# Identity products in TensorE's waits, the next norm inside the output part, and the last 64 rows by rows: a four-layer f32 attention kernel

## The chip, the cores and the metric

One core of a Trainium2 chip. The metric is the device time of the kernel in microseconds (us); all data are f32. Before the change the median of three runs is 2748.88 us (2748.11 to 2750.48).

The engines are called as the profile calls them: PE (TensorE, the matrix products; PEld is its weight load), DVE (VectorE), ACT (ScalarE), POOL (GpSimd), and SP, which in this kernel issues the DMAs in one queue. [...] A product of f32 operands is two matrix instructions (two passes) in the profile.

## The reference

Four layers work one after the other on `x` (8, 100, 512); each also reads the context `ctx` (8, 361, 512).

```python
x = gqa(x, ctx, mask)         # L0: 32 heads over 8 key heads, residual, layer norm
x = time_mix(x, ctx[:, ...])  # L1: norm, shift, five gated mixes, a scan over the 100 rows
                              #     (32 heads of 16x16 states), norm per head, residual;
                              #     then ln2, shift, and x + sigmoid(xr @ Wr) * (relu(xk @ Wk)**2 @ Wv)
x = x + alpha * attend(x, ctx, w_q, w_k, w_v, w_o)       # L2: one head of 512
for i in (1, 2):                                         # L3: two cross-attentions
    h  = layer_norm(x, ln_i)
    q  = h @ wq + bq                                     # 16 heads of 128
    k  = concat(ctx @ wk + bk, bias_k)                   # 361 + 1 keys
    v  = concat(ctx @ wv + bv, bias_v)
    w  = softmax(q k^T / sqrt(128))
    x  = x + (w v) @ wo + bo
x = x + gelu(layer_norm(x) @ w_fc1 + b_fc1) @ w_fc2 + b_fc2   # 512 -> 2048 -> 512
```

## The kernel before, in words

The first layer fills 0 to about 300 us of the profiled span, the second and third layer (interleaved, in units of two batches) 300 to 830, the last layer's cross-attentions 830 to 2570, its MLP the rest.

*Second and third layer.* PE's order is written by hand: generators (`prescan`, `mixing`, `after` and others) yield pieces, and an order of pieces is laid out so that one unit's products stand in another's waits. The rest of the engines are ordered by the tile scheduler from program order and readiness. `normed` (line 553) normalizes rows and turns them by products with the identity into a bank `pn`; `through` (line 598) takes a 512x512 weight through a bank `pp`; `prescan` takes the mix through `w1` into a bank `pt` (line 617). The scan is on DVE (`st<-wd,a`, 1.83 us each) and POOL.

*Last layer.* Four steps, (layer 1, 2) x (half 0, 1), a half being four batches, 400 columns. All engines are ordered by the scheduler. Each step has these parts:

- `project_queries` (L1160): for pairs of heads, `seven_products` (L1120, a two-by-two block product with seven instead of eight products, whose operands' sums are made beforehand on POOL and DVE and whose results are combined on DVE) gives `pq`, then q, and `through_keys` multiplies q by the head's key weight, so that `qz` holds 512 values for each of 16 heads x 100 rows = 1600 rows of a batch. The sums of the input `hT`, called `hs`, are four additions on DVE at its head (L1172 to 1175). While pair h is projected, pair h-2 goes through the keys (`some_keys`); in the first pair there is nothing for that place.
- `attend` per batch (L1212): 12 tiles of 128 rows in pairs, and 64 rows left. For a pair of tiles, `pair_of_scores` (L1272) makes sums `ss` on POOL (`sums`, L1237) and seven products with the context, then softmax on DVE and ACT, transposes, and `block_with_context` (L1289) multiplies by the context with seven products. The parts of the latter wait in a list (`waiting`) and are put between the scores' products (`meanwhile`). The last 64 rows of two batches share one softmax; `with_context` (L1247) multiplies each batch's 64 columns by the context with four column parts, three key blocks each, two to a bank `pz`, and evicts them to `qz` (L1342 to 1350).
- the next half's `normalize` (L1473): `take_rows` loads its four row blocks `xin`, statistics and normalization on DVE, transposes on PE (`pt<-ident,xhat`, line 128), ACT writes `hT`.
- `project_outputs` (L1390): first `take_rows` loads the rows to which the result is added. For pairs of heads, `pa` by the value weight, `u` (the value bias and the bias key's weight, loaded from `pd`) added on DVE into `aT`, POOL makes `sums` of `aT` and the output weights, and the pair before goes through the seven output products `po`, added on DVE to seven accumulators `acc` and `more` (L1425). After the last pair, the accumulators are added up (L1427), turned on PE (`pt<-ident,more`, line 1466), added to the rows on DVE (L1467), and stored by SP (`put_rows`).

PSUM banks and SBUF tiles rotate by tag; `l3_ctx` and `l3_out` are pools on the same side of SBUF, opened one after the other.

## Time and profile before

| what | value |
|---|---|
| median of the runs | 2748.88 us |
| the profiled execution's own time | 2747.97 us |
| its span, first to last instruction | 2745.9 us |
| mean granted clock of PE | 0.983 |
| PE busy | 2621.6 us, 95% |
| DVE busy | 1605.1 us, 58% |
| POOL busy | 1042.8 us, 38% |
| ACT busy | 935.8 us, 34% |

The busy shares are of the span. The row of clocks gives the TensorE clock granted in tenths of full speed, in 40 slices of 68.6 us. The waits of an engine are listed as `engine line waited for: us in total, times, longest us`. In a timeline, each line is start, duration, engine, line, operation, and in brackets the idle time before it with the instruction that ended it. A line of a table of stretches gives the stretch, its length, then busy time and count of PE, PEld, DVE, ACT and POOL, the mean granted clock, the DMA share and GB/s.

### The profile page before, as it was taken

The numbers are of one execution on the slowest core, as the hardware profiler recorded it, in microseconds if no ns is written. First come the engines' busy times: TensorE is split into PE (matmuls) and PEld (weight loads), VectorE is DVE, ScalarE is ACT, GpSimd is POOL, SyncE is SP. The second block draws the span as 40 slices with busy tenths as digits, with TensorE's granted clock in tenths as the row PEclk, the third lists the DMA queues.
The fourth block names the chain that finished last, engine by engine and source line by source line (L and its number), as shares of the span: only waits on it lengthen the run. The fifth ranks groups of instructions, "written<-read, shape, count | busy, mean of one in ns | idle before, by whom it ended". The sixth has DMA issues, their size and how long they took to land.

```text
span 2745.9 us, 40332 instructions
## 1 busy us (share of the span) xinstructions
PE 2621.6 (95%) x14356; PEld 2093.8 (76%) x14356; DVE 1605.1 (58%) x3995; ACT 935.8 (34%) x2143; POOL 1042.8 (38%) x1362
## 2 busy tenths in 40 slices
PE   8999888888989999999999999999999999999999
PEld 5666466666666888877788877789887788886688
DVE  4788366877524656546556546555554655654743
ACT  5777334543321333310233330243331143331121
POOL 2000144532204445355345446344546334535212
PEclk9999889999999999999999999999999999999999
DMA  7432333354205100045200035400015510005400
GB/s 228 119 102 74 121 110 123 94 151 121 81 26 154 51 23 23 7 130 161 78 23 23 1 91 149 127 19 23 12 38 147 148 43 23 23 7 162 155 13 13
DMA packets 149682, 220.63 MB, mean 80 GB/s; under 512 B 45302, under 2 KB 78646, under 8 KB 149226
## 3 DMA queue, kind: packets, MB, share of 16 engines
q1 hardware_dynamic: 149482, 218.05, 27.5%
q8 instruction: 114, 1.87, 0.3%
q14 instruction: 86, 0.70, 0.1%
HBM read 207.48 MB, written 10.53 MB: 79 GB/s over the span
## 4 chain that ended last, share of the span: by engine, by line
PE 67%; POOL 4%; DVE 3%; DMA 2%; issue 1%; ACT 1%; SPq 0%; DVEq 0%; POOLq 0%; ACTq 0%
PE pz L97 18%; PE sl L97 9%; PE pk L1168 6%; PE su L97 5%; PE pq L97 5%; PE po L1416 5%; PE pa L97 5%; PE pp L97 3%; PE pu L97 3%; PE pt L1336 2%; PE pl L97 2%; DMA xin<-xd 1%; PE sc L1377 1%; PE sc L97 1%; POOL ss L1241 1%
## 5 line engine op out<-in xcount | busy, mean ns | idle before, releaser
L97 PE MATMUL pz<-at,cr 121*128 121x256 f32 (+1 forms) x960 | 255.3, 378 | 0.0
L751 POOL TENSOR_TENSOR st<-st,r 128x800 f32<-128x800 f32 x64 | 111.8, 1748 | 233.5 <-DVE st L745 195.3
L1311 DVE TENSOR_TENSOR qz<-pz,qz 128x512 f32<-128x512 f32 x192 | 131.9, 687 | 113.7 <-PE pz L97 105.8
L97 PEld LDWEIGHTS pz<-at,cr 121*128 121x128 f32 (+1 forms) x960 | 177.5, 189 | 21.0
L1168 PE MATMUL pk<-q,wb 128*128 128x400 f32 x512 | 189.9, 501 | 3.1 <-issue 3.1
L97 PE MATMUL pa<-qz,wa 128*128 128x400 f32 x512 | 178.2, 499 | 0.1
L97 PE MATMUL sl<-ts,ss 128*128 128x181 f32 x768 | 156.5, 325 | 3.7 <-POOL ts L1233 0.2
L97 PE MATMUL pz<-at,cs 121*128 121x256 f32 (+1 forms) x576 | 149.7, 380 | 0.0
L1241 POOL TENSOR_TENSOR ss<-qz 128x256 f32<-128x256 f32 x96 | 69.8, 727 | 207.1 <-PE su L97 118.4
L97 PEld LDWEIGHTS pa<-qz,wa 128*128 128x128 f32 x512 | 96.2, 190 | 64.9 <-DVE aT L1454 0.9
L1091 ACT COPY qz<-pk 128x400 f32<-128x400 f32 x128 | 63.0, 492 | 236.0 <-PE pk L1168 236.0
L1339 ACT COPY at<-pt 121x384 f32<-121x384 f32 x192 | 84.2, 480 | 159.2 <-PE pt L1336 94.1
L1358 ACT ACTIVATE pr<-su,nm 128x362 f32<-128x362 f32 x96 | 54.1, 564 | 239.4 <-DVE nm L1354 239.3
L97 PEld LDWEIGHTS sl<-ts,ss 128*128 128x128 f32 x768 | 118.2, 190 | 21.3 <-issue 7.1
L1168 PEld LDWEIGHTS pk<-q,wb 128*128 128x128 f32 x512 | 93.6, 190 | 50.5 <-ACT qz L1091 3.7
L350 PEld LDWEIGHTS pt<-ident,pr 115*121 115x121 f32 (+1 forms) x672 | 83.2, 185 | 56.5 <-ACT at L230 29.2
L745 DVE TENSOR_TENSOR_SCAN st<-wd,a 128x808 f32<-128x808 f32 x64 | 117.0, 1828 | 14.7 <-PE py L756 12.9
L1361 ACT ACTIVATE pr<-pr,ss 128x362 f32<-128x362 f32 x200 | 113.5, 595 | 31.7 <-DVE ss L1359 31.6
L342 ACT ACTIVATE pr<-pr,nm 115x361 f32<-115x361 f32 (+1 forms) x224 | 115.2, 592 | 10.4 <-DVE nm L338 10.4
L97 PEld LDWEIGHTS pz<-at,cs 121*128 121x128 f32 (+1 forms) x576 | 104.4, 189 | 13.7 <-issue 1.8
L338 DVE CUSTOM_DVE_ANT_0 pr<-sc,mask 115x361 f32<-115x361 f32 (+1 forms) x224 | 106.0, 530 | 11.0 <-PE sc L326 10.8
L350 PE MATMUL pt<-ident,pr 115*121 115x115 f32 (+1 forms) x672 | 99.9, 280 | 11.0 <-ACT at L230 5.4
(383 smaller groups left out, 6241.1 us busy)
## 6 DMA issues: line engine op xcount, KB each, us to landing
va<-vd SPq DMA_DIRECT2D x64, 404.0 KB
wa<-in_L_xattn_wq SPq DMA_DIRECT2D x64, 256.0 KB
wb<-in_L_xattn_wk SPq DMA_DIRECT2D x64, 256.0 KB
wa<-in_L_xattn_wv SPq DMA_DIRECT2D x64, 256.0 KB
wb<-in_L_xattn_wo SPq DMA_DIRECT2D x64, 256.0 KB
u<-pd SPq DMA_DIRECT2D x64, 200.0 KB
cr<-in_ctxR SPq DMA_DIRECT2D x16, 726.0 KB
cx<-in_ctxT SPq DMA_DIRECT2D x16, 722.0 KB
```

The costliest lines, as they stand in the source:

```text
L97: nc.tensor.matmul(dst, lhsT=lt, rhs=r, start=(i == 0), stop=(i == len(pairs) - 1))
L338: nc.vector.tensor_tensor_reduce(out=pr[:n], in0=sc[:n, :S], in1=mk[t][:n], scale=-1.0, scalar=FLT_MAX, op0=ALU.add, op1=ALU.min, accum_ou ...
L342: nc.scalar.activation(pr[:n], pr[:n], AF.Exp, bias=nm[:n], scale=-1.0)
L350: nc.tensor.transpose(pt[:KB, k * n : (k + 1) * n], pr[:n, lo : lo + KB], ident[:n, :n])
L745: nc.vector.tensor_tensor_scan(st.rearrange("p q b l -> p (q b l)"), wd.rearrange("p q t -> p (q t)"), a, 0.0, ALU.mult, ALU.add,)
L751: nc.gpsimd.tensor_tensor(st, st, rc.unsqueeze(1).to_broadcast([P, 4, UB, L]), ALU.mult)
L1168: nc.tensor.matmul(pk[:, :HT], lhsT=wk[:, c * P : (c + 1) * P], rhs=q, start=True, stop=True)
L1241: nc.gpsimd.tensor_tensor(ss_[:, 0], rows[1][0], rows[1][1], ALU.add)
L1311: nc.vector.tensor_tensor(dst, pz, other, ALU.add)
L1339: nc.scalar.copy(at, pt[:KB, : 3 * TR].rearrange("p (k r) -> p k r", r=TR))
L1361: nc.scalar.activation(pr[:, : S + 1], pr[:, : S + 1], AF.Copy, scale=ss)
L1416: nc.tensor.matmul(po[:, c], lhsT=left[k][:, c * P : (c + 1) * P], rhs=right[k], start=True, stop=True)
```

## The change

Four things change.

1. `keep_busy(bank, n)` puts n products of the identity with itself (128x128) into a bank that the next products are about to overwrite. It is called at six places of PE's order: before the mix's products in `prescan` of unit 1 (11), in `through` of the third layer's queries of unit 1 (14), before the transposes of ln2 in `after` of units 2 and 3 (10 each), before `wfk` of the last unit (14), and before the first query products of the last layer (10).
2. The next half's normalization and its `hs` are made inside the output part, before the pair of heads 6, and the rows' loads are put behind it. The accumulators are one tile of seven parts; turning them, adding the rows and storing them is a function `rows(i)` that the next step calls in the two free places of its first seven products (the last step calls it before the MLP).
3. `ts_` is made before `cs`, and the sums `ss` of the next pair of tiles are made, in program order, right after this pair's products.
4. The last 64 rows of two batches go through the context as 64x512 products, rows by rows: the first batch in partitions 0 to 63 of one bank, the second in 64 to 127; ACT copies the bank, four 128x128 transposes turn it, two evictions write `qz`.

```diff
+    def keep_busy(bank, n):
+        for _ in range(n):
+            nc.tensor.matmul(bank[:, :P], lhsT=ident, rhs=ident, start=True, stop=True)
...
             pair = [bank("pn") for _ in range(2)]
+            keep_busy(pair[0], fill)
...
                 pp = bank("pp")
+                keep_busy(pp, 0 if h else fill)
...
             pt = bank("pt")
+            keep_busy(pt, 11 if u == 1 else 0)
...
+                if h == 0 and rows_of_last is None:
+                    keep_busy(banks[0], 10)
...
                 def some_keys(cs, ahead=ahead):
+                    if ahead is None:
+                        first_between(cs[0][0])
...
-            def with_context(i, cr, cs, at, r0):
-                n = at.shape[-1]
-                pz = ps.tile([P, 512], F32, tag="z", name="pz")
-                pz = pz[:, : 2 * n].rearrange("p (c n) -> p c n", c=2)
-                for k, c in enumerate(cs):
-                    mm_sum(
-                        pz[:, k],
-                        [
-                            (cr[:m, kb, c * P : (c + 1) * P], at[:m, kb])
-                            for kb, m in enumerate((KB, KB, S - 2 * KB))
-                        ],
-                    )
-                evict(qz[:, i, cs[0] : cs[0] + 2, r0 : r0 + n], pz)
+            def last_rows(at, crs):
+                held = []
+                def first():
+                    pz = ps.tile([P, 512], F32, tag="z", name="pl")
+                    for kb, m in enumerate((KB, KB, S - 2 * KB)):
+                        for q, cr in enumerate(crs):
+                            nc.tensor.matmul(
+                                pz[q * RR : (q + 1) * RR, :], lhsT=at[:m, kb, q * RR : (q + 1) * RR], rhs=cr[:m, kb, :],
+                                start=(kb == 0), stop=(kb == 2),
+                            )
+                    lr = pc.tile([P, 2, 2 * TR], F32, tag="u1", name="lr", bufs=1).rearrange("p i n -> p (i n)")
+                    nc.scalar.copy(lr, pz)
+                    held.append(lr)
+                def second():
+                    pz = ps.tile([P, 512], F32, tag="z", name="pl")
+                    for c in range(NC):
+                        nc.tensor.transpose(pz[:, c * P : (c + 1) * P], held[0][:, c * P : (c + 1) * P], ident)
+                    for q in range(2):
+                        evict(
+                            qz[:, i - 1 + q, :, NT * TR :],
+                            pz.rearrange("p (c r) -> p c r", c=NC)[:, :, q * RR : (q + 1) * RR],
+                        )
+                return [(part, 2 * TR) for part in (first, second)]
...
+                if t + 2 < NT:
+                    made[i, t + 2] = sums(i, t + 2)
+                elif i + 1 < HB:
+                    made[i + 1, 0] = sums(i + 1, 0)
...
-            take_rows(bs, po_, tag="xin", bufs=HB)
             ahead = None
             for h in range(0, NH, 2):
+                if h == 6:
+                    normalize_next()
+                    take_rows(bs, po_, tag="xin", bufs=HB)
...
-            for i, b in enumerate(bs):
+            def rows(i):
+                b = bs[i]
                 pt = ps.tile([P, 512], F32, tag="tp", name="pt")
                 for c in range(NC):
                     o = oT[c // 2][i // 2][:, c % 2, (i % 2) * L : (i % 2 + 1) * L]
                     nc.tensor.transpose(pt[:L, c * P : (c + 1) * P], o, ident)
                 nc.vector.tensor_tensor(x[b], pt[:L, :], x[b], ALU.add)
-            put_rows(bs)
+                put_rows([b])
...
+            def normalize_next():
+                nonlocal hT, blocks_of_hT
+                hT = normalize(*(("_mlp", 0) if last else steps[n + 1]), po_)
+                blocks_of_hT = None if last else token_blocks(hT)
+
+            rows_of_last = project_outputs(layer, half, pd, dv, po_, normalize_next)
+        for i in range(HB):
+            rows_of_last(i)
```

More of the change, by code (lines that the diff above doesn't have):

```diff
@@ L551, in split, with normed @@
             return t.rearrange("p c (b l) -> p c b l", l=L)
-        def normed(u, means, rs, scale, offset, out, kind, ahead=True):
+        def normed(u, means, rs, scale, offset, out, kind, ahead=True, fill=0):
             us = slice(u * UB, (u + 1) * UB)
@@ L596, in mixed_by, with through @@
                 nc.vector.scalar_tensor_tensor(m[:, c], sx[:, c], col(name, c), xu[:, c], ALU.mult, ALU.add)
-        def through(w, m, evict_to):
+        def through(w, m, evict_to, fill=0):
             for h in range(2):
                 pp = bank("pp")
+                keep_busy(pp, 0 if h else fill)
                 for i in range(2):
@@ L823, in after @@
             got = []
-            yield from normed(u, mv, rstd, "L1_xattn_ln2_w", "L1_xattn_ln2_b", got, 0)
+            yield from normed(
+                u, mv, rstd, "L1_xattn_ln2_w", "L1_xattn_ln2_b", got, 0, fill=10 if u > 1 else 0
+            )
             xu = got[0]
@@ L832, in after @@
             yield
-            yield from through(wfk, xk, lambda cs, pp: nc.scalar.activation(kk[:, cs], pp, AF.Relu))
+            yield from through(
+                wfk, xk, lambda cs, pp: nc.scalar.activation(kk[:, cs], pp, AF.Relu), 14 if u == NU - 1 else 0
+            )
             nc.gpsimd.tensor_tensor(kk, kk, kk, ALU.mult)
@@ L889, in mixing @@
             scale = 1.0 / float(np.sqrt(np.float32(C)))
-            yield from through(wqk, xT, lambda cs, pp: nc.scalar.activation(qk[:, cs], pp, AF.Copy, scale=scale))
+            yield from through(
+                wqk, xT, lambda cs, pp: nc.scalar.activation(qk[:, cs], pp, AF.Copy, scale=scale),
+                14 if u == 1 else 0,
+            )
             for add in rest:
@@ L1158, in right_sums, with token_blocks, project_queries @@
             eng.tensor_tensor(s[2], b[1][0], s[0], ALU.subtract)
-        def project_queries(layer, hT, added):
+        def token_blocks(hT):
+            b = [[hT[:, 2 * k : 2 * k + 2, n * HN : (n + 1) * HN] for n in range(2)] for k in range(2)]
+            hs = big.tile([P, 4, 2, HN], F32, tag="oT", name="hs")
+            hs = [hs[:, k] for k in range(4)]
+            right_sums(nc.vector, b, hs)
+            return b, hs
+        def project_queries(layer, hT_all, hT, added, first_between):
             ep, ahead = None, None
@@ L1169, in through_keys @@
                     evict(qz[:, :, c, h * L : (h + 1) * L], pk[:, :HT].rearrange("p (b l) -> p b l", l=L))
-            b = [[hT[:, 2 * k : 2 * k + 2, n * HN : (n + 1) * HN] for n in range(2)] for k in range(2)]
-            hs = big.tile([P, 4, 2, HN], F32, tag="oT", name="hs")
-            hs = [hs[:, k] for k in range(4)]
-            right_sums(nc.vector, b, hs)
+            b, hs = hT
+            hT = hT_all
             for h in range(0, NH, 2):
@@ L1209, in project_queries, with attend @@
             return ep, late
-        def attend(b, i, ep, pd, waiting, turning, pc, loaded):
+        def attend(b, i, ep, pd, waiting, turning, pc, loaded, made):
             cT = pc.tile([P, NC, S + 1], F32, tag="cT", name="cT")
@@ L1218, in attend @@
             loaded.append((cT, cr))
+            bs = [[cT[:, 2 * k : 2 * k + 2, j * SH : (j + 1) * SH] for j in range(2)] for k in range(2)]
+            ts_ = pc.tile([P, 4, 2, SH], F32, tag="ts", name="ts", bufs=1)
+            nc.gpsimd.tensor_tensor(ts_[:, 0], bs[0][1], bs[0][0], ALU.subtract)
+            nc.gpsimd.tensor_tensor(ts_[:, 1], bs[1][1], ts_[:, 0], ALU.subtract)
+            nc.gpsimd.tensor_tensor(ts_[:, 2], bs[1][1], bs[0][1], ALU.subtract)
+            nc.gpsimd.tensor_tensor(ts_[:, 3], bs[1][0], ts_[:, 1], ALU.subtract)
             cs = pc.tile([KB, 5, 2 * P], F32, tag="cs", name="cs", bufs=1)
@@ L1227, in attend, with sums @@
             nc.gpsimd.tensor_tensor(cs[:, 4], a[0][2], a[1][2], ALU.subtract)
-            bs = [[cT[:, 2 * k : 2 * k + 2, j * SH : (j + 1) * SH] for j in range(2)] for k in range(2)]
-            ts_ = pc.tile([P, 4, 2, SH], F32, tag="ts", name="ts", bufs=1)
-            nc.gpsimd.tensor_tensor(ts_[:, 0], bs[0][1], bs[0][0], ALU.subtract)
-            nc.gpsimd.tensor_tensor(ts_[:, 1], bs[1][1], ts_[:, 0], ALU.subtract)
-            nc.gpsimd.tensor_tensor(ts_[:, 2], bs[1][1], bs[0][1], ALU.subtract)
-            nc.gpsimd.tensor_tensor(ts_[:, 3], bs[1][0], ts_[:, 1], ALU.subtract)
-            def sums(t):
+            def sums(i, t):
                 rows = [[qz[:, i, 2 * k : 2 * k + 2, r * TR : (r + 1) * TR] for k in range(2)] for r in (t, t + 1)]
@@ L1245, in sums @@
                 return rows, ss_
-            def with_context(i, cr, cs, at, r0):
-                n = at.shape[-1]
-                pz = ps.tile([P, 512], F32, tag="z", name="pz")
-                pz = pz[:, : 2 * n].rearrange("p (c n) -> p c n", c=2)
-                for k, c in enumerate(cs):
-                    mm_sum(
-                        pz[:, k],
-                        [
-                            (cr[:m, kb, c * P : (c + 1) * P], at[:m, kb])
-                            for kb, m in enumerate((KB, KB, S - 2 * KB))
-                        ],
-                    )
-                evict(qz[:, i, cs[0] : cs[0] + 2, r0 : r0 + n], pz)
+            def last_rows(at, crs):
[7 more added lines that the diff above has]
+                                start=(kb == 0), stop=(kb == 2),
+                            )
+                    lr = pc.tile([P, 2, 2 * TR], F32, tag="u1", name="lr", bufs=1).rearrange("p i n -> p (i n)")
[9 more added lines that the diff above has]
+                            pz.rearrange("p (c r) -> p c r", c=NC)[:, :, q * RR : (q + 1) * RR],
+                        )
+                return [(part, 2 * TR) for part in (first, second)]
             def meanwhile():
@@ L1272, in pair_of_scores @@
             def pair_of_scores(t):
-                rows, s = sums(t)
+                rows, s = made.pop((i, t)) if (i, t) in made else sums(i, t)
                 banks = [ps.tile([P, 512], F32, tag=g, name=n)[:TR] for g, n in (("sc", "su"), ("mm", "sl"))]
@@ L1295, in block_with_context @@
                 t = pc.tile([KB, 3, 2 * TR], F32, tag="bt", name="bt", bufs=1)
-                u1 = pc.tile([P, 2, 2 * TR], F32, tag="u1", name="u1", bufs=1)
+                us = []
                 nc.gpsimd.tensor_tensor(t[:, 1], b[1][1], b[0][1], ALU.subtract)
@@ L1317, in second @@
                 def second():
+                    u1 = pc.tile([P, 2, 2 * TR], F32, tag="u1", name="u1", bufs=1)
+                    us.append(u1)
                     plus(u1, product([(cs[:, 1], t[:, 0])]), c12)
@@ L1322, in third_ @@
                     pz = product([(cs[:, 0], b[0][1]), (a[1][2][:third], b[2][1][:third])])
-                    plus(c12, pz, u1)
+                    plus(c12, pz, us[0])
                     plus(c22, pz, c21)
@@ L1344, in turn_rows @@
                         waiting.extend(block_with_context(part, r0))
-                        continue
-                    waiting.extend(
-                        (lambda i=i, cr=cr, part=part, r0=r0, cs=cs: with_context(i, cr, cs, part, r0), n)
-                        for cs in ((0, 1), (2, 3))
-                    )
+                if len(parts) == 2:
+                    waiting.extend(last_rows(at, [cr for _, cr, _, _ in parts]))
             def softmax(sc, e, at, parts):
@@ L1388, in attend, with project_outputs @@
                     softmax(sc, NT * HB + i // 2, at, parts)
-        def project_outputs(layer, half, pd, dv, po_):
-            acc = big.tile([P, 4, 2, HN], F32, tag="oT", name="acc")
-            more = po_.tile([P, 4, 2, HN], F32, tag="acc", name="more", bufs=1)
-            acc = [acc[:, 0], more[:, 0], acc[:, 1], acc[:, 2], more[:, 1], more[:, 2], more[:, 3]]
+        def project_outputs(layer, half, pd, dv, po_, normalize_next):
+            acc = po_.tile([P, 7, 2, HN], F32, tag="acc", name="acc", bufs=1)
+            acc = [acc[:, k] for k in range(7)]
             bo = [col(f"L3_xattn_bo{layer}", c) for c in range(NC)]
@@ L1467, in project_outputs @@
                 nc.vector.tensor_tensor(x[b], pt[:L, :], x[b], ALU.add)
-            put_rows(bs)
+                put_rows([b])
+            return rows
         def normalize(layer, half, rows):
@@ L1480, with first_between @@
         hT = third[3]
+        blocks_of_hT = token_blocks(hT)
+        rows_of_last, at_outputs = None, ExitStack()
         for n, (layer, half) in enumerate(steps):
             wx, ch, dv = added[layer]
+            def first_between(k):
+                if rows_of_last is not None:
+                    rows_of_last(2 * k)
+                    rows_of_last(2 * k + 1)
+                if k:
+                    at_outputs.close()
+            ep, late = project_queries(layer, hT, blocks_of_hT, (wx, ch), first_between)
             at_right = ExitStack()
             pc = at_right.enter_context(tc.tile_pool(name="l3_ctx", bufs=2, side="right"))
-            ep, late = project_queries(layer, hT, (wx, ch))
             pd = dram.tile([HB, ROWS], F32, tag="pd", name="pd")
             waiting, turning = [(part, 2 * TR) for part in late], []
-            loaded = []
+            loaded, made = [], {}
             for i in range(HB):
-                attend(half * HB + i, i, ep, pd, waiting, turning, pc, loaded)
+                attend(half * HB + i, i, ep, pd, waiting, turning, pc, loaded, made)
             for part in turning:
@@ L1495 @@
             at_right.close()
-            if n == len(steps) - 1:
+            last = n == len(steps) - 1
+            if last:
                 pw1 = ctx.enter_context(tc.tile_pool(name="mlp_w1", bufs=1, side="right"))
                 w1 = [load(pw1, "L3_xattn_w_fc1", NC, C, f"fc1_{k}", lo=k * C) for k in range(2)]
-            with tc.tile_pool(name="l3_out", bufs=2, side="right") as po_:
-                hT = normalize(*(steps[n + 1] if n + 1 < len(steps) else ("_mlp", 0)), po_)
-                project_outputs(layer, half, pd, dv, po_)
+            at_outputs = ExitStack()
+            po_ = at_outputs.enter_context(tc.tile_pool(name="l3_out", bufs=2, side="right"))
+            def normalize_next():
[5 more added lines that the diff above has]
+            rows_of_last(i)
+        at_outputs.close()
     FF = 2048
```

## The prediction

> **What bounds the kernel.** I began with the page's busy shares, the clock row and the chain that ended last.

> ```profile
> span 2745.9 us, 40332 instructions
> PE 2621.6 (95%) x14356; PEld 2093.8 (76%) x14356; DVE 1605.1 (58%) x3995; ACT 935.8 (34%) x2143; POOL 1042.8 (38%) x1362
> ...
> PEclk9999889999999999999999999999999999999999
> ...
> PE 67%; POOL 4%; DVE 3%; DMA 2%; issue 1%; ACT 1%; SPq 0%; DVEq 0%; POOLq 0%; ACTq 0%
> ```

> TensorE is the bound nearly throughout; only its work, its gaps and its clock can move the time. No engine beside it is above 58%. The clock is below full in layers two to three alone, so next come TensorE's waits there.

> ```profile
> PE pn L577 <- ACT xhat L564: 6.6, 4, 3.4
> ...
> PE pp L97 <- DVE v L858: 4.6, 2, 4.1
> PE pp L97 <- DVE y L596: 3.7, 1, 3.7
> ...
> PE pq L97 <- DVE hs L1156: 3.1, 1, 3.1
> PE pt L97 <- DVE mix L596: 3.1, 1, 3.1
> ```

> These hold the six places with added products: gaps of 3.10 us (at 371.7), 4.06 (626.4), 2.68 (700.7), 3.36 (774.4), 3.72 (779.4) and 3.11 (830.4). The table by stretches shows what follows (busy us of each engine; the third number from the right is the granted clock).

> ```profile
> 371.00:376.00 5.00, 1.80 (x12) 1.45 (x13) 4.62 (x6) 1.66 (x3) 3.37 (x4) 0.57 0.51 134
> ...
> 631.00:637.00 6.00, 6.00 (x35) 5.54 (x34) 3.35 (x4) 2.30 (x5) 1.74 (x1) 0.72 0.28 79
> ...
> 705.00:711.00 6.00, 6.00 (x20) 5.41 (x19) 1.01 (x1) 3.18 (x8) 1.14 (x1) 0.62 0.00 0
> ...
> 779.00:785.00 6.00, 2.28 (x9) 1.97 (x8) 2.36 (x7) 1.75 (x4) 1.68 (x2) 0.50 0.00 0
> ```

> The trace's clock records step between 1.0 and 0.5, always in lengths that are multiples of 3.41 us. In the last layer (830 to 2570 us) the clock is full, and the timeline shows where TensorE still waits: at the head of an output part, and where the next step begins.

> ```profile
> 1184.52 4.87 PE L97 MATMUL pa<-qz,wa 128*128 128x400 f32 x14
> 1191.17 0.56 PE L128 MATMUL pt<-ident,xhat 100*128 100x100 f32 x4 [1.78 <-DVE xhat L109]
> 1191.91 0.56 PE L128 MATMUL pt<-ident,xhat 100*128 100x100 f32 x4 [0.19 <-DVE xhat L109]
> ...
> 1267.18 0.64 PE L1466 MATMUL pt<-ident,more 128*100 128x128 f32 x4 [0.67 <-DVE more L1427]
> ...
> 1271.87 2.32 PE L97 MATMUL pq<-hs,wqs 128*128 128x200 f32 x12 [0.83 <-DVE hs L1156]
> ```

> Last, the products that the change re-forms:

> ```profile
> 979.55 2.65 PE L1377 MATMUL sc<-cT,qz 128*64 128x361 f32 x16
> ...
> 993.28 1.67 PE L97 MATMUL pz<-last,cr 121*128 121x64 f32 x14
> 994.79 0.83 PE L97 MATMUL sl<-ts,qz 128*128 128x181 f32 x4
> ```

> **The change, part by part.** Every f32 product is two passes on TensorE; the counts below are passes.

> *Last 64 rows.* Before, 48 passes of 64 columns per pair of batches; the 14 above occupy 994.79 − 993.28 = 1.51 us, 0.108 each, so 5.20 us. After: 12 passes of 512 columns, eight transpose passes, one copy on ACT and two evictions for four. At 400 columns a pass is (4.87 − 0.50)/13 = 0.336 us, so 512 columns are 0.430. Were they one after another: 5.16, plus eight transposes of 128 columns at 0.109 (the three at 991.72 are followed 0.33 us later) = 0.87, together 6.03: a loss of 0.83, times eight pairs +6.6 us. But they go alternately to partitions 0–63 and 64–127 of the result. The row `sc<-cT,qz`, with the same alternation, does 16 passes of 361 columns in 2.65 − 0.47 (one pass's own length) = 2.18 us over 15 starts; 361 columns alone are 0.303, so two share one slot. If all twelve pair up: 2.58 + 0.87 = 3.45, a gain of 1.75 (−14.0 in all). The built order puts the first product alone, then scores, then the other five: 0.86 + 3 slots of 0.86 + 0.87 = 4.31. I take this, the nearest row with the built order: 0.89 × 8 = **−7.1** (ends −14.0, +6.6). The transposes wait for ACT's copy, which queues behind two exponentials; from the product's end I reckon 3.6 us to the copy's end against 3.9 us until TensorE comes to them, so no wait, with 0.3 us to spare. Fewer evictions relieve ACT and DVE, which are not the bound: nothing. The shared buffer of that copy (u1) is next written by a later block's part: nothing; without that cover, one copy (0.5 us) per pair, 4 us, inside the ends.

> *Normalizing inside the output part.* In the first three steps the head loses 1.78 + 0.19 us here and about 1.66 and 2.00 (+0.2 each) in the next two: 6.0. After, its transposes stand after the second group of output products, statistics are made on DVE in the first microseconds, and only the third and fourth rows' normalization is done in place, under one 400-column product; I leave 0.2 per step: **−5.5** (ends −6.5, 0). In the fourth step the head also shows 1.42, 0.28, 0.77, 0.19 and 1.55 us of waits, since the row loads share the queue with two 1-MB weight loads; the normalization's 0.96 goes and the row loads are issued later: **−2** (−5, 0). On SP the second four row loads now stand partly behind output weights, two of them waiting for the last normalized rows; the weight loads queued behind them are for a pair of heads one pair later, about 10 us ahead (85 us over eight pairs), which covers a wait of some microseconds. DVE's four sums `hs` move from the next start into the part, where DVE has half its time free (5.08 of 10 us busy at its end).

> *Rows of the result in the next step's start.* 0.67 (transposes on the sums' end) and 0.83 (first products on `hs`) go; a third, 1.05 us between query and key products, I leave. 1.50 × 3 = **−4.5** (ends −7.6 with the third, 0 if the four additions on DVE, 0.68 us each in the rows of before, come before the query sums that TensorE needs next). SP's row stores move behind one query weight: the next use is an output part away. Around the MLP's start: nothing, a fraction of 0.8 us.

> *Identity products.* An identity product is two passes of 0.109, 0.218 us: 11 are 2.40, 14 are 3.05, 10 are 2.18 us, each shorter than its gap at full clock; cover is the gap, and at half clock they last 4.4 to 6.1 us and would delay the work by 1.3 to 2.4 us. Half-speed costs half of TensorE's busy time in it; by the clock records the stretches behind the six gaps cost 1.9, 1.7, 3.1, 3.2 and 2.7 us (the fourth and fifth gap share one): 12.6 is the ceiling. In these records a 3.41-us window with about 2 us idle is followed by half clock. The 3.06-us gap at 486.5 was not followed by one, since it fell across two windows; where the windows fall in another run I cannot know. At the first place half clock begins 0.04 us into the gap and so stems from the earlier 1.92-us wait: there the products run at half clock and cost time. I take **−6** (ends −12.6, +4).

> [...]

> *Order in layer two.* The built order lets a `mix` on DVE come one or two scan steps (1.8 us each) later around 385 us, where `pm` already waits 5.2 us in all: **+1** (0, +4).

> *Sums sooner.* The list in program order changes; in the built order POOL's `ss` stands at the same places with the same waits. About 35 of 76 changes of pair keep their 0.25-us wait on it: **0** (ends −9, 0).

> Sum: −7.1 − 5.5 − 2 − 4.5 − 6 + 1 = −24.1 on the profiled 2747.97 us (2.1 of it around the span) = 2723.9. The median of the runs shown is 0.9 above that execution: **2724.8 us**, −0.9%.

> **Rivals.** *(a) Fills don't keep the clock.* For: the first place, and windows whose position I don't know. Against: the other five gaps begin at full clock. Then +4 stands for −6: 2735.
> *(b) Accumulating half-width products do not overlap*, or the copy on ACT comes late. For: only `sc`, without a third accumulation step, shows overlap. +6.6 for −7.1: 2738.5.
> *(c) Slower: SP's queue starves the output part.* A row load that waits for the last normalized rows holds all weight loads behind it. For: it is one queue, and these loads wait on DVE. If the hold outlasts the 10-us lead, TensorE stands; a whole lead lost in four steps is 40, 2765. It decides from (24 + 5.5)/4 = 7.4 us per step on. Against: the four weight buffers of the next heads stand ahead in the queue, and before, all four rows' transposes lie within 1191 to 1195.
> *(d) Nothing arrives*: DVE, at 9 of 10 us busy at the next start, and POOL (`sums`) set the pace of these stretches, and only overlaps move: about 2747.

> **How the numbers follow.** What this kernel's runs can tell from no change is about 0.2%, 5.5 us. Chances: forecast (2707 to 2731) 0.52; (a) 0.18; (b) 0.12, both faster; (c) 0.09; (d) 0.05; gains larger than my range 0.04. (d) I split 0.04 same, 0.01 faster. Faster 0.52 + 0.18 + 0.12 + 0.04 + 0.01 = 0.87, same 0.04, slower 0.09. The range 2705 to 2746 holds forecast, (a), and (b) with part of its spread, leaving out (c), half of (d), and tails.

> **What will show it.** Right: no `pt<-ident,xhat` wait over 0.5 us; no `hs` wait at 1264, 1698 and 2131 (shifted); `pl<-cr,last` twelve passes in about 3.4 us with starts in pairs; PEclk at 1.0 after five of the six gaps. Wrong: pairs of `pl` starting 0.43 apart (b); identity products 0.22 us apart at clock 0.5 (a); `pa` waiting for `wa` or `sums` for `wb` mid-part (c). The forecast also fails if the ACT copy makes `pt`-like transposes of `lr` wait, or if the 0.25-us waits on `ss` vanish.

## The result

The changed kernel takes 2729.74 us (median of six runs, 2724.82 to 2739.3) against 2749.68 us (six runs, 2748.11 to 2753.84): a ratio of 0.9927, 95% interval 0.991 to 0.9943. The forecast was 2724.8 with a range of 2705 to 2746. The profiled executions took 2747.97 and 2728.69 us. Two later executions of the kernel before, of 3479.35 and 6371.63 us, were in a slow state and enter no comparison.

The page of the changed kernel, the lines that answer to those shown of before:

```profile
span 2726.9 us, 40045 instructions
...
PE 2623.8 (96%) x14238; PEld 2073.3 (76%) x14238; DVE 1602.7 (59%) x3987; ACT 939.1 (34%) x2143; POOL 1042.5 (38%) x1362
...
PEclk9999888999999999999999999999999999999999
```

TensorE is as busy as before (2621.6 then) in a span 19 us shorter. The clock's row has not become better. TensorE's waits in layers two and three, and then in the last layer with the MLP (us in total, times, longest):

```profile
PE pn L583 <- ACT xhat L569: 7.6, 4, 5.9
PE pm L642 <- DVE mix L650: 7.0, 7, 2.8
PE pp L102 <- DVE y L849: 3.6, 1, 3.6
```

```profile
PE pt L133 <- DVE xhat L114: 2.5, 1, 2.5
PE pz L97 <- POOL bt L1341: 1.8, 4, 0.5
PE pt L1510 <- DVE acc L1467: 1.7, 3, 0.8
PE pq L97 <- POOL wqs L1166: 1.3, 2, 1.1
```

The last layer's waits on `hs` (2.5 us) and between query and key products (3.1) are gone, and of those on `xhat` (7.0, eight times) one of 2.5 us stands, at a place that had none before. In layers two and three a 5.9-us gap stands where 2.7 were, and line 102, the identity products, is itself in the list as one that waits.

To see where the time went, I took each TensorE instruction that two traces share and the difference of its start to the start in before; the table has the median of these differences within 6 us of a place of before's span (negative: earlier than before). The programs without identity products (e1, e3, e4) have before's instructions, in before's order, up to 858 us.

| kernel | 300 | 412 | 622 | 672 | 760 | 858 | 2440 | 2545 | 2700 |
|---|---|---|---|---|---|---|---|---|---|
| changed | −0.9 | −0.8 | −0.2 | 1.0 | 4.7 | 0.4 | −17.6 | −20.5 | −19.0 |
| changed, once more (g4) | −1.0 | 2.0 | 6.7 | 9.5 | 13.7 | 15.9 | −3.7 | −6.3 | −4.7 |
| no products (e1) | −1.1 | −2.1 | 3.2 | 0.6 | −0.4 | −1.7 | −20.4 | −22.8 | −21.7 |
| rows alone (e3), no products | −0.7 | −1.3 | 0.1 | 0.4 | 0.4 | 0.4 | 0.3 | 0.1 | −0.1 |
| norm inside alone (e4), no products | −0.8 | 0.6 | 6.0 | 3.4 | 2.4 | 1.1 | −12.0 | −15.1 | −15.7 |
| last three places (e2) | −0.1 | 0.0 | 5.4 | 4.4 | 3.0 | −0.4 | −19.6 | −24.1 | −22.9 |

The whole gain lies in the last layer and its MLP: from 858 to 2700 us the changed kernel gains 19.4 us, and from the first layer's end to 858 us it loses 1.3 (0.4 + 0.9). Run again, it gains 20.6 in the first stretch and loses 16.9 in the second.

### The profile page after: what moved, and what is told of

The parts are those of the page before. It is cut to its first block, busy times and chain, and to the rows that moved or that the text cites. A ratio compares the mean times of both kernels' runs of the same rounds, so it can differ in the third digit from the quotient of the medians.

```text
span 2726.9 us, 40045 instructions
## 1 busy us (share of the span) xinstructions
PE 2623.8 (96%) x14238; PEld 2073.3 (76%) x14238; DVE 1602.7 (59%) x3987; ACT 939.1 (34%) x2143; POOL 1042.5 (38%) x1362
## 4 chain that ended last, share of the span: by engine, by line
PE 68%; POOL 4%; DVE 3%; DMA 1%; issue 1%; ACT 1%; SPq 0%; DVEq 0%; POOLq 0%; ACTq 0%
PE pz L97 16%; PE sl L97 9%; PE pk L1190 6%; PE su L97 6%; PE pa L97 5%; PE pq L97 5%; PE po L1456 5%; PE pp L97 3%; PE pu L97 3%; PE pt L1380 2%; PE pl L97 2%; PE pl L1279 1%; DMA xin<-xd 1%; PE sc L1418 1%; PE sc L97 1%
## 5 line engine op out<-in xcount | busy, mean ns | idle before, releaser
L97 PE MATMUL pz<-at,cr 121*128 121x256 f32 (+1 forms) x960 | 255.9, 378 | 0.0
L97 PEld LDWEIGHTS pz<-at,cr 121*128 121x128 f32 (+1 forms) x960 | 177.2, 189 | 20.8
L97 PE MATMUL pa<-qz,wa 128*128 128x400 f32 x512 | 178.1, 500 | 0.0
L97 PE MATMUL sl<-ts,ss 128*128 128x181 f32 x768 | 156.7, 326 | 3.7
L97 PE MATMUL pz<-at,cs 121*128 121x256 f32 (+1 forms) x576 | 149.8, 380 | 0.2 <-DVE qz L1353 0.2
L97 PEld LDWEIGHTS pa<-qz,wa 128*128 128x128 f32 x512 | 95.9, 190 | 64.4 <-DVE aT L1496 0.6
L97 PEld LDWEIGHTS sl<-ts,ss 128*128 128x128 f32 x768 | 118.5, 190 | 21.8 <-issue 7.1
L1465 DVE TENSOR_TENSOR acc<-po,acc 128x400 f32<-128x400 f32 x196 | 111.4, 572 | 15.1 <-PE po L1456 0.5
L97 PEld LDWEIGHTS pz<-at,cs 121*128 121x128 f32 (+1 forms) x576 | 104.4, 189 | 14.1 <-issue 1.6
```

What stands on the lines that cost most here:

```text
L97: nc.tensor.matmul(dst, lhsT=lt, rhs=r, start=(i == 0), stop=(i == len(pairs) - 1))
L1465: nc.vector.tensor_tensor(acc[k], po, acc[k], ALU.add)
```

## The experiments

### First series: the products, and each other part alone

**e1, no identity products.**

```diff
-        for _ in range(n):
+        for _ in range(0):
```

> The changed kernel without the 69 identity products. Theory A (from the changed kernel's trace, mine now): two of the six places cost time (the bank is held until 0.5 us before the real products at the second; the third stands in no wait at all), two gain, so together they give about nothing: 2726 to 2731 us against 2729.7 with them, with half clock back behind the waits at about 774 to 790 and 830. Rival B (the prediction's term): the products are worth 6 us, so 2736.

Measured: 2726.28 us (2725.29 to 2732.3), ratio to before 0.9923 (0.991 to 0.9935). The products at six places aren't worth 6 us: with them the kernel is 3.5 us slower by the medians and 1 by the ratios, and the intervals overlap.

**e2, products at the last three places only** (11 of `prescan`, 14 of the queries and 10 of unit 2's ln2 set to 0).

```diff
-            keep_busy(pt, 11 if u == 1 else 0)
+            keep_busy(pt, 0)
...
-                u, mv, rstd, "L1_xattn_ln2_w", "L1_xattn_ln2_b", got, 0, fill=10 if u > 1 else 0
+                u, mv, rstd, "L1_xattn_ln2_w", "L1_xattn_ln2_b", got, 0, fill=10 if u > 2 else 0
...
-                14 if u == 1 else 0,
+                0,
```

> Identity products only at the last three of the six places (ln2 of the last unit, wfk of the last unit, first query products of the last layer). Theory A: the first three cost about 2 + 2.4 + 3.7 us in the profiled run, so 2722 to 2725. Rival B (every place holds the clock for what follows): taking three away loses 1 to 4 us, 2731 to 2734.

Measured: 2724.65 us (2723.7 to 2727.81), ratio 0.9913 (0.9899 to 0.9926). On theory A's side of the two, though its interval overlaps that of e1.

Why the first three places fail is in the changed kernel's timeline; here are the second and the third.

```profile
629.83 5.02 PE L102 MATMUL pp<-ident 128*128 128x128 f32 x28 [3.57 <-DVE y L849]
634.69 2.87 PE L97 MATMUL pp<-v,w 128*128 128x200 f32 x16
```

```profile
691.75 2.40 PE L102 MATMUL pn<-ident 128*128 128x128 f32 x20
693.99 0.85 PE L583 MATMUL pn<-ident,xhat 100*128 100x100 f32 x8
```

At the second place the products waited 3.57 us of the gap for their bank, which DVE was yet to empty (`y`, line 849), and ran then, for two thirds at half clock (631.07 to 634.48): the real products start at 634.69, though their `v` was done at 630.74, and 4.19 us behind before's 630.50. They then take 2.87 us instead of before's 4.65, which ran mostly at half clock (631.10 to 634.52), so that not all of the delay is lost: from 622 to 672 us the changed kernel loses 1.2 us, and 2.8 when it was run again. At the third place the 2.40 us were put before ln2 of unit 2, and no TensorE gap ends there: before's gap at 700.7 belongs to the *last norm's second unit*, as its ACT output `hT` tells; ln2 writes `xu`. So they are added work. DVE's order changed as well: a scan (1.80 us) now stands ahead of the reciprocal and of `nb`, which the next norm needs, and the gap at 703 grew from 2.68 to 5.90 us. In e2, without the first three places' products, it is 2.68 us again; which of the three moved the scan was not tried. From 672 to 760 us the changed kernel loses 3.7 us, and 4.3 when it was run again (g4). At the first place, the products ran mostly at half clock, as feared, 368.64 to 372.62 (half clock from 368.24 to 371.65).

At the fourth and fifth, the products did what they should (stretches of the changed kernel; the clock is the third number from the right):

```profile
779.00:785.00 6.00, 4.73 (x43) 4.35 (x42) 1.89 (x5) 3.26 (x7) 0.00 (x0) 1.00 0.00 0
785.00:791.00 6.00, 5.26 (x37) 4.95 (x36) 2.79 (x8) 0.58 (x2) 1.68 (x2) 1.00 0.00 0
```

Before's clock was 0.50 and 0.74 there. All nine traces with these products (the changed kernel's two, e2, f1 to f4, g1, g3) gain 2.6 to 2.7 us from 760 to 800 us; of the four traces without (e1, e3, e4, g2) none gains more than 0.9.

From 800 to 858 us, the nine lie between 1.7 us of gain and 6.8 of loss. Two waits, of 1.23 and 0.58 us, near 814 us in before, stand in all fourteen traces. By the clock records, which change at multiples of 3.413 us, at least 1.76 us of them fell within one such window in the changed kernel's second run, f1, f2, g1 and g2, and half clock followed for three or four windows. In the other nine traces a window's end parts them, with at most 1.63 us on one side, and none followed. The stretches behind these waits in f1 and in the changed kernel:

```profile
815.80:826.00 10.20, 9.74 (x45) 9.08 (x44) 0.37 (x1) 1.20 (x3) 0.00 (x0) 0.50 0.01 2
```

```profile
818.80:829.00 10.20, 9.55 (x60) 7.29 (x61) 0.45 (x2) 1.47 (x4) 0.00 (x0) 1.00 0.01 2
```

So from 760 to 858 us the changed kernel gains 4.3 us in its first trace and loses 2.2 in its second; e2 gains 3.3. Without products e1 and e4 gain 1.3 each, e3 nothing, and g2 (below) loses 4.6. Of the sixth place these runs show nothing: half clock begins behind it in one of the nine traces (g1), but in e1 and e4 in neither.

**e3, the last 64 rows by rows alone**: the kernel before, with `last_rows` for `with_context`.

> The kernel before with the last 64 rows by rows and nothing else. Theory A: about 0.7 to 0.8 us less per pair of batches in the timeline, eight times, so 6 us less: 2743.5. Rival B (ACT's copy and the stalls between the twelve passes eat it where nothing else moves): 2748 to 2750. All of it must lie in the last layer; up to 830 us nothing moves.

Measured: 2748.04 us (2737.55 to 2759.71), ratio 0.9992 (0.9973 to 1.0012): rival B's number, but not for its reason. The interval reaches from 7.4 us less to 3.3 more, so that the medians alone don't exclude a gain of 6. In the trace every pair of batches takes 0.66 to 0.81 us less, 5.9 in eight. The table has none of it at 2440 us, because the three output parts' heads lose it again. The timeline of e3 there, and its clock:

```profile
1190.02 0.56 PE L128 MATMUL pt<-ident,xhat 100*128 100x100 f32 x4 [1.88 <-DVE xhat L109]
...
1191.16 2.82 PE L97 MATMUL pa<-qz,wa 128*128 128x400 f32 x4
```

```profile
1190.00:1200.00 10.00, 9.80 (x48) 7.85 (x49) 2.86 (x5) 7.64 (x23) 4.64 (x7) 0.83 0.53 151
```

The wait is much the same as before's 1.78 us, but it has moved within the clock's windows: in before a window ends at 1190.89, with 1.50 us of the wait ahead of that, and the clock stays full; in e3 the 1.88 us and the 0.19 behind them all lie in the 3.413 us ahead of 1191.3, and `pa` behind them takes 2.82 us for 1.53. The clock records have half clock at 1191.3, 1624.8 and 2058.2 us, each for 3.4 us. These are 433.5 and 433.4 apart, 127 times 3.413: a step of this kernel is nearly a whole number of windows long, so the three heads lie at nearly the same place of a window, and here all three were hit. Each cost 1.4 us or more.

**e4, the next norm inside the output part alone** (with the rows in the next start; no products, `with_context` back, sums as before).

> The changed kernel without identity products, with the last 64 rows as before and the sums as before: only the next norm inside the output part and the result's rows in the next step's start are left. Theory A: 4.3 us per step from the two places, 12 in three steps, and 1 to 2 in the fourth: 2735 to 2737. Rival B (the move pays only together with shorter attends): 2743 or more.

Measured: 2733.44 us (2731.98 to 2736.88), ratio 0.9945 (0.9931 to 0.9958): better than theory A's number. From 858 to 2700 us it gains 16.8 us. This part carries the change, and it also takes away the wait that e3 stumbles over. That the rows do pay beside it, e1 shows, which has them and the new order of the sums: 3.2 us less than e4 from 858 to 2700 us, and 7.2 in the medians. The timeline of the changed kernel in the next step's start:

```profile
1261.19 1.52 PE L97 MATMUL pq<-hT,wa 128*128 128x200 f32 x8
1262.54 0.84 PE L97 MATMUL pq<-hs,wqs 128*128 128x200 f32 x4
1263.22 0.38 PE L1510 MATMUL pt<-ident,acc 128*100 128x128 f32 x2
1263.90 0.86 PE L1510 MATMUL pt<-ident,acc 128*100 128x128 f32 x6 [0.29 <-DVE acc L1467]
```

TensorE goes from output to query products without a gap, and of 2.55 us of waits at this place 0.29 is left.

### Second series: the waits that were left

**f1, the copy apart.** The prediction put a 0.25-us wait, some 35 times, down to POOL's sums `ss`. In the changed kernel's trace 33 of 76 places have it, and there the third score product (`sl<-ts,ss`) starts 0.14 to 0.20 us after the end of ACT's copy `tu<-sl` of the *first* product, which lies in the same bank. The sum `ss` that this product reads was done 7 us earlier or more at all 33; the sums that end near its start are the next pair's. One place on TensorE and on ACT:

```profile
1015.69 0.78 PE L97 MATMUL sl<-cT,qz 128*128 128x181 f32 x4
1016.30 0.78 PE L97 MATMUL su<-cT,qz 128*128 128x181 f32 x4
1017.17 0.85 PE L97 MATMUL sl<-ts,ss 128*128 128x181 f32 x4
```

```profile
1016.63 0.20 ACT L1399 ACTIVATION_READ_ACCUMULATOR pr<-su,nm 128x1 f32 x1
1016.73 0.30 ACT L1145 COPY tu<-sl 128x181 f32<-128x181 f32 x1
```

The copy stands behind the end of an exponential on ACT and ends at 1017.03. At all 33 it begins 0.26 us after its product, against 0.04 at the 43 places without a wait. At 21 of the 33 the third product starts 0.143 to 0.145 us after the copy's end, as it does at 35 of the 43 without a wait. At the other 12, each the first pair of a batch, it starts 0.19 to 0.20 us after the copy's end but 0.053 or 0.054 after POOL's sum `ts` of the context, which it also reads, and which the profile names as what ended the wait. One of the 12 on TensorE, ACT and POOL:

```profile
1037.34 0.88 PE L97 MATMUL sl<-ts,ss 128*128 128x181 f32 x4
```

```profile
1036.84 0.30 ACT L1145 COPY tu<-sl 128x181 f32<-128x181 f32 x1
```

```profile
1036.39 0.90 POOL L1248 TENSOR_TENSOR ts<-cT,ts 128x362 f32<-128x362 f32 x1
```

So 21 waits (5.3 us) end with ACT's copy and 12 (3.6 us) with POOL's `ts`, there only some 0.05 us later than the copy would have allowed; none is for `ss`. The edit, on e2's kernel, puts a context part between the second and third score product:

```diff
             product(c11, 1)
             nc.vector.tensor_tensor(c11, c11, tu[:, 0], ALU.add)
+            if len(between) > 2:
+                between[2]()
             product(c21, 2)
...
-                def first():
-                    meanwhile()
-                    turn_waiting()
...
-                    tu, (first, meanwhile),
+                    tu, (turn_waiting, meanwhile, meanwhile),
```

> The kernel with products at the last three places only, and in each pair of scores one waiting context part put between the second and the third of the seven score products instead of behind the third. Theory A: the 0.25-us wait ahead of the third product is for ACT's copy of the first product's block, which lies in the same bank (in the trace it ends 0.14 to 0.20 us before TensorE goes on): the waits at these places fall from about 10 us in all to 2 or less, and the time by up to 8 us against products at the last three places (2716 to 2720), unless a wait behind the third product (for DVE's sum from that bank) takes their place. Rival B (the prediction's: the wait is for POOL's sums ss): the 0.25 us stay, whatever stands between: 2724.

Measured: 2713.08 us (2711.09 to 2714.38), ratio 0.9865 (0.9849 to 0.9882), better than theory A's number. The time ahead of `sl<-ts,ss` beyond the length that the instruction before it takes at TensorE's pace (0.61 us from `su<-cT,qz` at 987.33 to the next start, where nothing waits) is 10.9 us in all in before, in the changed kernel and in e2, and 0.6 in f1. From 858 to 2545 us f1 gains 33.5 us on before, e2 23.7. The run alone can't tell ACT's copy from POOL's sums, since the work in between hides either; which engine ended which wait rests on the distances in the changed kernel's trace. This version beats both kernels.

**f2, the MLP's second half normalized later** (on e2's kernel).

```diff
+                for _ in norm:
+                    pass
...
-                    next(norm, None)
+                    if j >= 2:
+                        next(norm, None)
```

> Products at the last three places only, and the MLP's second half is normalized two weight pairs later. Theory A: the changed kernel's new wait of 2.49 us for the normalized rows at 2572, and the half clock behind it (2576.7 to 2580.1), are made by the normalization coming while its rows are still loading; later they are there: 2.5 us of wait and 1.7 us of half clock go, the wait of 2.1 us for the weights of before may come back: 2 to 4 us less, 2721 to 2723. Rival B (the wait moves along, since DVE is full in that stretch): 2724 to 2725.

Measured: 2725.13 us (2723.18 to 2727.05), ratio 0.991 (0.9896 to 0.9925): rival B's number. The wait moved along and is 1.99 us; in this trace no half clock follows it, which is worth 2 us at this place (−0.8 from 2545 to 2700 us, against +1.2 in e2), but the median doesn't show it. The edit didn't bring that about: e4, without it, has a wait of 2.10 us there and no half clock, and f4, with it, has half clock at 2567.9.

**f3, ten products for the gap at 700.7, in the wrong unit** (on e2's kernel, in `last_norm`, `10 if u == 0`).

> Products at the last three places and ten more before the transposes of the last norm's first unit, where before had its 2.68-us gap (the changed kernel had put them before ln2 of unit 2, where no gap was). Theory A: in a real gap, with its bank free, products keep the next window's clock: no half clock at about 703 to 713, 1.7 to 3 us less in that stretch than the changed kernel without them. Rival B: the bank is taken too, or the windows fall otherwise: half clock there as before, or the transposes 2 us late.

Measured: 2723.34 us (2720.54 to 2734.43), ratio 0.9914 (0.9893 to 0.9935). My mistake was the change's own: unit 0's transposes stand at 733, where there is no gap. The products ran from 731.07 to 733.30, and the stretch from 672 to 760 us lost 2.3 us, their length.

**f4, the three edits together.**

> The three edits of this series together. Theory A: their gains add, 10 to 14 us under products at the last three places alone: 2711 to 2716. Rival B: the waits move on: 2720 to 2725.

Measured: 2716.08 us (2711.64 to 2720.54), ratio 0.9877 (0.9858 to 0.9895): not better than f1 alone. f3's products cost, f2's edit gives nothing, and in this profile half clock fell on 2137.8 and 2479.1 us.

### Third series: the right gap

**g1, ten products in the second unit's norm** (on e2's kernel, `10 if u == 1`).

> Products at the last three places, and ten more before the transposes of the last norm's second unit, which is the 2.68-us gap of before at 700.7 (the run before this one had put them in the first unit's, at 731, where no gap was: there they cost 2.2 us). Theory A: they start within 0.3 us of the gap's beginning, end before the rows are there, and the half clock at about 703 to 710 is gone: 2 to 3 us less in the timeline by 750 than with products at the last three places. Rival B: half clock stays or the transposes come late: no gain.

Measured: 2723.87 us (2722.4 to 2727.45), ratio 0.9906 (0.9885 to 0.9926). At the place itself theory A is right about the clock; the timeline and the stretch of g1, and the same stretch of e2, where the gap is at 705:

```profile
701.31 2.40 PE L102 MATMUL pn<-ident 128*128 128x128 f32 x20
704.16 1.27 PE L583 MATMUL pn<-ident,xhat 100*128 100x100 f32 x8 [0.45 <-ACT xhat L569]
```

```profile
709.00:715.00 6.00, 6.00 (x33) 3.89 (x32) 3.88 (x5) 0.86 (x2) 0.21 (x1) 1.00 0.12 34
```

```profile
709.00:715.00 6.00, 6.00 (x24) 4.73 (x23) 1.01 (x1) 3.61 (x8) 1.57 (x1) 0.83 0.00 1
```

The clock stays full, and from 672 to 760 us the kernel gains 2.7 us, as g3 (below) does with the same products. The traces without products there gain 0.0 to 1.5 us in that stretch, e2 1.5, so that against e2 it is 1.2 and not the 2 to 3 expected. But at 812.7 and 840.0 us half clock falls on a stretch that e2 had at full clock, and 4.1 us are lost again by 858 us; the first of these is behind the two waits near 814 us described above. The median is e2's.

**g2, the copy apart and no products at all; g3, the copy apart, the last three places and the right gap; g4, the changed kernel once more.**

> The changed kernel without any identity product, with the context part put ahead of the third score product. Theory A (the products are worth little, 0 to 4 us by where the clock's windows fall): 2713 to 2718 against 2713 with the last three places. Rival B (prediction's 6 us): 2719 or more.

> The context part ahead of the third score product, products at the last three places and in the real gap at 700.7: the best that theory A knows, 2710 to 2713. Rival B: as g2, 2713 to 2718.

> The changed kernel once more, on the chip of the three others. All theories: 2724 to 2735, and 12 to 16 us over the kernel that has the context part ahead of the third score product and products at the last three places.

Measured: g2 2714.85 us (2710.14 to 2723.29), ratio 0.9873 (0.9851 to 0.9895); g3 2713.85 us (2705.89 to 2719.98), ratio 0.9874 (0.985 to 0.9898); g4 2731.45 us (2724.91 to 2743.05), ratio 0.9939 (0.9915 to 0.9963). Products at the best places I know or none: the same in the medians. What they are worth in all is less than these runs can tell apart, 2 us or so either way, although at three places the traces show it each time. Between the changed kernel, run again, and f1, g2, g3 lie 17 to 18 us in the medians, a little over the 12 to 16 expected; f1's trace gives 10 of them to the waits ahead of the third score product, and the rest I can only lay to the three places that cost and to the windows.

**Sums sooner** has no run of its own. In e1, which has the new order of the sums, POOL's instructions stand in before's order for the first 365 of them, to 1190 us, which is through the scores of the first four batches; beyond that it is not shown.

## Why the prediction was right, and where not

The number fell inside the range, about midway between the forecast (2724.8) and rival (a)'s 2735, so the number alone decides nothing between them; the terms do.

- *Normalizing inside, and the rows in the next start*: −10.0 in three steps and −2 in the fourth. Measured in the changed kernel, less 0.7 to 0.8 per pair of batches: −4.3, −2.7 and −5.1, together −12.1, and −2.9 in the fourth. I had left the 1.05 us between query and key products where it was; it went too (3.1 us in before's list, none after). The −4.5 should have been its end of −7.6. Rival (c), SP's queue, didn't come: no wait on `wa` stands in the list.
- *The last 64 rows*: −7.1. Measured −5.9. The products of the two batches do run side by side (starts at 996.163 and 996.170, 996.643 and 996.650), so rival (b) is out. The twelve passes take 1.01 + 2.72 us, not 3.44. They stand as predicted, the first product's two passes and the last two alone and the others in pairs, but in each of the two groups the first pass takes 0.48 us and the last 0.52 instead of 0.43, and the way into a group costs 0.24 us where it cost 0.15 in before. The four transposes are four passes, not eight, and take 0.43 us; I had counted two for each. ACT's copy ended at 999.58 and the transposes came at 1000.22, so it held up nothing.
- *Identity products*: −6. This term failed: instead of a gain, the changed kernel loses 1.3 us from 300 to 858 us in one trace and 16.9 in the other, and without the products it is no slower (e1). That is nearer to rival (a)'s +4. Rival (a) had its ground in windows of unknown position, and the result does scatter: four traces of before's instructions reach 858 us between 1.7 us ahead of before's own trace and 10.2 behind it. For the first three places the runs showed plainer causes: a window that was slow already, a bank that is not yet free, and a place that isn't the one with the gap. At the fourth and fifth the term was sound, 2.6 us in each trace. The last cause was in my reach: I gave the gap at 700.7 to ln2 by its line, and its ACT output `hT` would have told that it is another norm.
- *Order in layer two*: +1. From 360 to 412 us the changed kernel loses 2.2 and 2.7 in its two traces and the programs without products 1.2 to 1.4, so about +1; the reorder came from the products at the first place, since without them DVE's order is before's.
- *Around the MLP*: nothing. It costs 1.5 us in this trace: TensorE waits 2.49 us for the second half's norm, which now comes earlier, and half clock follows from 2576.7 to 2580.1. The 2.1-us wait for weights of before is gone in its place. Where no half clock follows the same wait (e4, f2), the stretch gains 0.6 to 0.8 instead, so I lay the loss to the 3.4 us at half clock. DVE begins the norm 0.73 us late, for the rows' load, and is then busy without a break until the norm is done. In f2 it begins 0.66 us late and the wait stays; how much of it is the load's and how much that of DVE's other work is open. I had seen these transposes come earlier in the built order and priced nothing.
- *Sums sooner*: 0, which holds as far as the order shown above goes, but none of the waits that I named was on `ss`: 21 of 33 ended with ACT's copy, 12 with POOL's `ts`.

The sum for the last layer with the MLP was −19.1 and is −19.4: rows and MLP worse by 1.2 and 1.5, the rest better by 3. What is missing of the predicted −24.1 is what layers two and three didn't give: +1.3 instead of −5, in part offset by 0.9 us up to 300 us, where nothing was changed. That the total came within 5 us of the forecast is partly luck: the second trace of the same kernel is 14 us longer than the first, all of it from ahead of 858 us.

## What to carry to other kernels

Work that only keeps TensorE busy must start when the gap starts: at the second place it began 3.57 us into the gap, and the products behind it 4.19 us later than before's; in g1 it began with the gap, at 701.31, and the clock stayed at 1.00. See in the trace that its bank is free then, and find the gap's owner by the tile that its results go to, not by a line that several callers share; other engines' work may change its order with it (DVE's scan at 704 us). When an engine waits right after a sum becomes ready, look at every operand's and every bank's last user before naming the cause, and ask which pair the sum belongs to: at 20 of 33 places a sum of POOL ended within 0.02 us of TensorE's going on, and it was the next pair's. The same distance at every place, 0.144 us from the copy or 0.053 from `ts`, told the cause. And a step whose length is near a multiple of the clock's window (433.5 us, 127 times 3.413) can repeat its luck: e3's gain of 5.9 us vanished since half clock followed the same wait three times. A median can hide a gain that the traces show at its place, if half clock then falls on a later stretch: g1 gained 2.7 us by 760 us and lost 4.1 by 858.

## What the runs showed of the hardware

No single length of idle time decides. Of the 3.413-us windows of before's trace at full clock, nine have TensorE idle for 1.96 us or more, and half clock follows all nine; it also follows windows with 1.83, 1.53, 1.25, 1.14 and 1.13 us (381.9, 655.0, 525.3, 320.5 and 457.0), but not those with 1.80 and 1.77 (2054.5 and 487.7). Near 814 us, 1.76 us within a window was followed by half clock (g2), and 1.96 us within the window from 828.4 us was not (e1). Waits of 1.88 and 0.19 us, 0.56 apart, were followed by it (e3, 1191.3), and so was a gap of 2.68 us (before, 0.62 over 705 to 711), until products filled it (g1, 1.00 from 697 to 715).

Passes whose results go to partitions 0 to 63 and 64 to 127 ran side by side in the changed kernel: the four pairs of `pl<-cr,last` from 996.163 start 7 to 11 ns apart, 0.43 to 0.48 us from pair to pair, and each pass takes 0.59 to 0.64 us.
